# Four graph-transformer layers on one core: sums of the second MLP moved between engines, degrees and a first column read earlier, and branches laid out the other way

## The chip, the cores and the metric

One core of a Trainium2 chip runs the whole program. The metric is the device time of one execution in microseconds. The median of three runs is 3004.81 us (3003.51 to 3010.91). Another execution, of 3007.94 us, was taken by the hardware profiler; all durations come from it. The engines are TensorE (PE; its weight loads are PEld), VectorE (DVE), ScalarE (ACT), GpSimd (POOL) and SyncE (SP, which issues transfers). A name with q (DVEq) is the engine's sequencer, that is, its branches and semaphores.

## The reference

1250 nodes have 512 features; 20,000 edges go from `src` to `dst`. Four layers follow one another; each adds to `x` a graph aggregation and a mixer of the normalised `x`, and then a feed-forward stage of 8 experts with two per node. Layer 0, which the change is about:

```python
xn = _layernorm(x)
x  = x + gnn(xn, edges) + mix(xn)          # mix: 2 x (linear attention; MLP)
x  = x + moe(_layernorm(x))                # gate_w: softmax, top 2 of 8 experts, shared expert
# gnn: deg counts the edges out of a node, plus its loop; dis = rsqrt(deg)
#      relu(segment_sum(dis[row] * dis[col] * (xn @ W.T + b)[row], col))
# mix, MLP i:  y = layernorm(x);  x = x + gelu(y @ W1[i] + b1[i]) @ W2[i] + b2[i]     # 512 -> 2048 -> 512
```

The layers that divide by the incoming degree need its inverse too, which the program computes once, in layer 0.

## The kernel before, in words

**Tiling.** The nodes are ten tiles of 125 rows (`NT`, `TP`), or three chunks of 500, 500 and 250 (`CH`). Everything is float32; matmuls of the aggregation take float32r pairs of a value and its rest.

**The graph.** POOL writes the number of edges between each pair of nodes into DRAM (`adj`) by accumulating transfers during layer 0. `Graph.arrived(t)` (L638 to L647) reads tile t of it into one buffer `at` (L642; issued by POOL), sums its rows to the outgoing degree `degO` on DVE (L643), and adds the tile to `into` on POOL (L645 for the first, L647 for the rest). There is one `at`, so the next read waits until both readers are done. `degrees()` (L649 to L667) makes a flag `heavy` (is any degree over 4096?), the incoming degree `degI` of each node by 20 small matmuls, and its inverse as a row in DRAM: three matmul groups with a row of ones (L664), three clamps and reciprocals on one partition (L665, L666), and three transfers by SP (L667). `inv_sqrt_deg` (L669) makes `dis`, and then the node features `hs` are scaled by it tile by tile on ACT (L1404) and split in two (`parted`, L676).

**The second MLP** is `l0_mlp(1, ..., roomy=False)` (L1205 to L1368), from 957 to 1222 us. It goes in 12 turns: four units of 512 hidden features by three chunks. All but the first turn's hidden product are products of two by two blocks done in seven half-size products (`seven`, L1175; a Strassen-Winograd scheme). `right_sums` (L1168 to L1173) forms four sums of the input's halves, `tx`, for each following turn (11 times, since there is no room to keep them; its other use, on W2, forms `t`). In `seven`, ACT copies three of the products out of PSUM (L1185), two sums are made on DVE (L1194, L1195), and the other products go to four outputs. Of the output products, `outputs` (L1311) adds a kept product to the running `xn` on DVE, and `add_to` (L213) adds the product in PSUM on DVE too. At the end of each turn `aside()` runs one piece of the graph's work, in this order (`steps`): five pieces of two `arrived` each, five pieces of scaling two tiles, then `degrees()`. The program order of each engine is what the source's order and a few pinned places make it; each engine takes its instructions in order.

**Behind the MLP.** `Columns` (L709) reads two tiles' columns of the counts at a time (five reads; the first of them in a pool of its own) by SP. After the MLP, SP issues the first read, then the reads of `x`, with further columns between them, then two weights, and `Arrival` (L462) reads the gate's weights `gw` (L473). `l0_gnn` (L863) then begins with `over` and takes ten tiles: gather by PE, DVE (L868), ACT (L869), DVE (L870), POOL (L871), and the norm and gate of the tile before (L486 to L497).

**Branches.** `over` (L745), called once in each of the four layers, is the path for counts that float32r can't hold: it loads the flag into each engine (L748) and branches (L749) over a body that never runs with this data. Its body's length differs by layer and engine. `Experts.run` has one such branch per layer too (L413), for more tiles of experts than usual. In the built program every engine first compares and, where the flag is 0, jumps over the body to an else block, which sets semaphores for those that wait for the body, and from there goes on.

Of the kernel before, what the change touches and what calls it, by code (L numbers as in the profile page):

```python
# [19 lines left out]
P = 128  # L20
# [4 lines left out]
E = 8  # L25
# [32 lines left out]
def gps_d4_kernel(ctx: ExitStack, tc: tile.TileContext, a: dict, out: bass.AP):  # L58
# [301 lines left out]
    class Experts:  # L360
# [45 lines left out]
        def run(self, to, use, last=lambda: None):  # L406


            self.to = to
            use(range(self.often), self.each(0, self.often))  # L410
            last()
            used = nc.values_load(self.exi[0:1, NLOAD:NLOAD + 1], min_val=2 * NPAIR, max_val=NTI)
            with tc.If(used > self.often + NPAIR):  # L413
                self.most = NLOAD
                self.start()
                use(range(self.often, NLOAD), self.each(self.often, NLOAD))
# [45 lines left out]
    class Arrival:  # L462

        def __init__(self, n, gate, xT=None, hidden=None):

            self.scope = ExitStack()
            self.pool = pool = self.scope.enter_context(tc.tile_pool(name="arrival", bufs=1, side="right"))
            self.rows = dram.tile([T, D], F32, name=f"rows{n}")  # L470
            self.k = gate.shape[0] // P
            self.gw = pool.tile([P, self.k, E], F32, name="gw")
            nc.sync.dma_start(self.gw, gate.rearrange("(c p) e -> p c e", p=P))  # L473
            self.xT, self.hidden = xT, hidden
            self.ps = bank()
            self.turned = None
# [76 lines left out]
    class Graph:  # L553
# [84 lines left out]
        def arrived(self, t):  # L638

            order = tc.keep_in_program_order  # L640
            at = self.at
            move(nc.gpsimd, at, adj[t * TP * T:(t + 1) * TP * T, :].rearrange("(p d) o -> p (d o)", d=T))  # L642
            order(nc.vector.tensor_reduce(degO[:, t:t + 1], at, AX.X, OP.add))  # L643
            if t == 0:
                nc.gpsimd.tensor_copy(self.into, at)  # L645
            else:
                nc.gpsimd.tensor_tensor(self.into, self.into, at, op=OP.add)  # L647

        def degrees(self):  # L649
            most = S.small.tile([TP, 1], F32, tag="most", name="most")  # L650
            nc.vector.tensor_reduce(most, degO, AX.X, OP.max)
            ps = bank()
            nc.tensor.transpose(ps[:1, :TP], most, ident[:TP, :TP])
            one = S.small.tile([1, 1], F32, tag="one", name="one")
            nc.vector.tensor_reduce(one, ps[:1, :TP], AX.X, OP.max)
            nc.vector.tensor_scalar(heavy, one, 4096.0, None, op0=OP.is_gt)
            ps = bank()
            for d in range(NT):
                mm(ps[:TP, d:d + 1], [(self.into[:, tok(d)], ones[:TP, 0:1])])
            nc.vector.tensor_copy(degI, ps[:TP, :NT])  # L660
            for c0, cn in CH:
                ps = bank()
                mm(ps[:1, :cn], [(ones[:TP, 0:1], self.into[:, c0:c0 + cn])])
                inv = S.small.tile([1, 500], F32, tag="inv", name="inv", bufs=1)  # L664
                nc.vector.tensor_scalar(inv[:, :cn], ps[:1, :cn], 1.0, None, op0=OP.max)  # L665
                nc.vector.reciprocal(inv[:, :cn], inv[:, :cn])  # L666
                nc.sync.dma_start(inv_row[:, c0:c0 + cn], inv[:, :cn])  # L667

    def inv_sqrt_deg(deg, r):  # L669

# [71 lines left out]
        nc.sync.dma_start(inv, bass.AP(tensor=inv_row.tensor, offset=inv_row.offset, ap=[[0, P], [1, T]]))  # L742
        return inv

    def over(use, rows=None, xn=None, given=None):  # L745


        some = nc.values_load(heavy[0:1, 0:1], min_val=0, max_val=1)  # L748
        with tc.If(some > 0):  # L749
            W = 500 if rows is None else TP  # L750
            with tc.tile_pool(name="over", bufs=1) as pool:
                more = [given(pool)] if given is not None else []

                def rest(s, c0, cn):
                    at = pool.tile([TP, W], F32, tag="at", name="at")
                    nc.sync.dma_start(at[:, :cn], counts()[:, s, c0:c0 + cn])
                    hi = pool.tile([TP, W], I32, tag="hi", name="hi")
                    nc.vector.tensor_scalar(hi[:, :cn], at[:, :cn].bitcast(I32), -4096, None, op0=OP.bitwise_and)
                    lo = pool.tile([TP, W], F32R, tag="lo", name="lo")
                    nc.vector.tensor_tensor(lo[:, :cn], at[:, :cn], hi[:, :cn].bitcast(F32), op=OP.subtract)  # L760
                    return lo

                def flags(s, k):
                    return dict(start=(s == 0 and k == 0), stop=(s == NT - 1 and k == 1))

                if rows is not None:
                    for d in range(NT):
                        ps = bank()
                        for s in range(NT):
                            lo = rest(s, d * TP, TP)  # L770
                            for k in range(2):
                                nc.tensor.matmul(ps[:TP, :], lo, rows[:, s, k, :], **flags(s, k))
                        use(d, ps[:TP, :])
                for c0, cn in CH if rows is None else []:
                    for f in range(NC):
                        part = part_feature(pool, xn, f, "part")
                        ps = bank()
                        for s in range(NT):
                            lo = rest(s, c0, cn)
                            for k in range(2):  # L780
                                nc.tensor.matmul(ps[:, :cn], part[:, s, k, :], lo[:, :cn], **flags(s, k))
                        use(f, c0, cn, ps[:, :cn], *more)
# [78 lines left out]
        return yT, z  # L861

    def l0_gnn(columns, rows, dis, hs, xn):  # L863
        over(lambda d, ps: add_to(hs[:, d, :], ps), rows=rows)
        for t in range(NT):
            ps = columns.gather(t, rows)
            u = S.small.tile([TP, D], F32, tag="u", name="u")
            nc.vector.tensor_tensor(u, ps, hs[:, t, :], op=OP.add)  # L868
            nc.scalar.activation(u, u, AF.Relu, scale=dis[:, t:t + 1])  # L869
            nc.vector.tensor_tensor(x[:, t, :], x[:, t, :], u, op=OP.add)  # L870
            nc.gpsimd.tensor_tensor(x[:, t, :], x[:, t, :], xn[:, t, :], op=OP.add)  # L871
            arrival[0].step(t)
        arrival[0].step(NT)
# [291 lines left out]
        v.tensor_tensor(o[:, 2], a12, o[:, 1], op=OP.subtract)  # L1165
        v.tensor_tensor(a21, a11, a21, op=OP.subtract)

    def right_sums(o, b11, b12, b21, b22, last=None):  # L1168
        v = nc.vector
        v.tensor_tensor(o[:, 0], b12, b11, op=OP.subtract)  # L1170
        v.tensor_tensor(o[:, 1], b22, o[:, 0], op=OP.subtract)
        v.tensor_tensor(o[:, 2], b21, o[:, 1], op=OP.subtract)
        v.tensor_tensor(b12 if last is None else last, b22, b12, op=OP.subtract)  # L1173
# [31 lines left out]
    def l0_mlp(i, xm, yT, front, then=None, aside=lambda: None, roomy=True):  # L1205

        b2 = row_bc(a["L0_mix_b2"][i])
        H2 = D // 2
        with tc.tile_pool(name=f"mlp{i}", bufs=1) as mp:
            tx = mp.tile([P, 4, 2, T // 2], F32, name="tx") if roomy else None  # L1210

            class Unit:
# [20 lines left out]
            def sums(u, c0, cn):  # L1233
# [3 lines left out]
                if u == 0:  # L1237
                    front.need(c0 + cn)
                if u == 0 or not roomy:
                    right_sums(t, yT[:, 0:2, left], yT[:, 0:2, right], yT[:, 2:4, left], yT[:, 2:4, right], t[:, 3])  # L1240
                return t

            def rests(u, k):
# [53 lines left out]
            def outputs(unit, c0, cn, hT):  # L1297
# [4 lines left out]
                for j in range(n // TP):  # L1302
# [5 lines left out]
                    def out(q):  # L1308
                        def f(ps, more=None):
                            if more is not None:  # L1310
                                nc.vector.tensor_tensor(parts[q], parts[q], more, op=OP.add)  # L1311
                            add_to(parts[q], ps)
                        return f

# [55 lines left out]
    def layer0_mixers():  # L1370
# [3 lines left out]
        with tc.tile_pool(name="l0a", bufs=1) as pool:  # L1374
# [16 lines left out]
            with tc.tile_pool(name="gnn", bufs=1) as gp:  # L1391
                rows = gp.tile([TP, NT, 2, D], F32R, name="hs2")
                dis = S.small.tile([TP, NT], F32, tag="dis", name="dis")
                with tc.tile_pool(name="columns", bufs=1) as cp:
                    graph.fetch(cp)

                    def steps():
                        for t in range(NT):
                            graph.arrived(t)
                            if t % 2:  # L1400
                                yield
                        inv_sqrt_deg(degO, dis)
                        for t in range(NT):
                            tc.keep_in_program_order(nc.scalar.mul(hs[:, t, :], hs[:, t, :], dis[:, t:t + 1]))  # L1404
                            parted(rows[:, t, 0, :], rows[:, t, 1, :], hs[:, t, :])
                            if t % 2:
                                yield
                        graph.degrees()
                        yield

                    pieces = steps()
                    l0_mlp(1, xn, yT, second[1], None, lambda: next(pieces, None), roomy=False)
                    with tc.tile_pool(name="columns2", bufs=1) as cp2:
                        columns = Columns(cp2, cp)
                        columns.fetch(pinned=True)
                        x = ctx.enter_context(tc.tile_pool(name="rows", bufs=1, side="right")).tile([TP, NT, D], F32, name="x")
                        load_x(nc.sync, x, True, lambda **k: columns.fetch(**k))
                        soon["L0"] = [load_w(a["L0_ffn_sw1"], pinned=True), load_w(a["L0_ffn_sw2"], pinned=True)]
                        arrival[0] = Arrival(0, a["L0_ffn_gate_w"], xnT)
                        l0_gnn(columns, rows, dis, hs, xn)  # L1420

    SQD = 512.0 ** 0.5
# [797 lines left out]
```

## Time and profile before

| quantity | value |
|---|---|
| median of three runs | 3004.81 us (3003.51 to 3010.91) |
| profiled execution, and its span | 3007.94 us, 3006.2 us |
| granted clock of PE, mean | 0.952 |
| second MLP | 957 to 1222 us |
| `arrived` reductions (L643) | 973.7 to 1076.4 us |
| first matmul behind the first general-path branch | 1227.54 us |
| branches L749 | near 1223, 1596, 2384 and 2703 us |
| L413, four branches | 1406 to 2964 us |

A line of groups gives the line of the source, engine, operation, output and inputs (partitions x elements), how often, and then busy time in total, mean ns of one, idle time of the engine just before, and what ended most of it. A line of waits reads: engine, tile and line that waited, `<-` what came last, total us, times, longest us. A line of windows gives the stretch, its length, the busy time of each engine with the number of its instructions, the granted clock, the busy share of the DMA engines and GB/s. The view of one source line gives each operation's count, minimum, median and maximum ns, and the start of the first and last, and then who waited for that line. "ns" there, us elsewhere.

### The profile page before, as it was taken

The numbers are of one execution on the slowest core, as the hardware profiler recorded it, in microseconds if no ns is written. First come the engines' busy times: TensorE is split into PE (matmuls) and PEld (weight loads), VectorE is DVE, ScalarE is ACT, GpSimd is POOL, SyncE is SP. The second block draws the span as 40 slices with busy tenths as digits, with TensorE's granted clock in tenths as the row PEclk, the third lists the DMA queues.
The fourth block names the chain that finished last, engine by engine and source line by source line (L and its number), as shares of the span: only waits on it lengthen the run. The fifth ranks groups of instructions, "written<-read, shape, count | busy, mean of one in ns | idle before, by whom it ended". The sixth has DMA issues, their size and how long they took to land. (4 is left out here: it accounts for less than half of the span.)

```text
span 3006.2 us, 33629 instructions
## 1 busy us (share of the span) xinstructions
PE 2753.6 (92%) x12041; PEld 1876.9 (62%) x12041; DVE 1421.4 (47%) x3477; ACT 763.0 (25%) x1715; POOL 673.0 (22%) x496
## 2 busy tenths in 40 slices
PE   7999999999999999889999978999799998889893
PEld 4457778865586878656475556667454657545562
DVE  6835677673356887444541550000324135443523
ACT  3233333342233333120211531111131022320010
POOL 3444444444000300042310001000201002032123
PEclk9999999999999999899999988999899998999897
DMA  8411112111000210638620018775340016651296
GB/s 238 122 15 15 3 29 47 29 33 15 15 15 24 87 45 15 161 108 263 164 77 1 21 35 300 249 239 195 94 132 15 1 35 207 204 145 44 61 317 196
DMA packets 248445, 301.59 MB, mean 100 GB/s; under 512 B 105258, under 2 KB 142509, under 8 KB 248247
## 3 DMA queue, kind: packets, MB, share of 16 engines
q1 hardware_dynamic: 137303, 208.28, 22.2%
q0 software_dynamic: 97408, 66.17, 9.7%
q10 hardware_dynamic: 13536, 24.65, 2.2%
q8 instruction: 106, 1.74, 0.2%
q14 instruction: 92, 0.75, 0.1%
HBM read 253.68 MB, written 44.91 MB: 99 GB/s over the span
## 5 line engine op out<-in xcount | busy, mean ns | idle before, releaser
L627 POOL DMA_INDIRECT adj<-count,cell x160 | 323.7, 2023 | 356.6 <-DMA adj<-count,cell 319.7
L187 PE MATMUL ps<-xnT,w 128*128 128x500 f32 (+1 forms) x832 | 311.7, 528 | 4.0 <-DVEq L749 3.3
L187 PE MATMUL ps<-w,hT 128*128 128x512 f32 (+1 forms) x592 | 264.7, 596 | 3.8 <-ACT hT L1504 3.8
L187 PE MATMUL ps<-w,xnT 128*125 128x512 f32 x560 | 251.5, 598 | 1.5 <-ACT xnT L1657 1.5
L187 PEld LDWEIGHTS ps<-xnT,w 128*128 128x128 f32 x832 | 158.2, 193 | 143.6 <-issue 133.2
L187 PE MATMUL ps<-xgT,w 128*128 128x256 f32 (+1 forms) x1256 | 235.8, 346 | 2.6 <-issue 1.8
L187 PEld LDWEIGHTS ps<-xgT,w 128*128 128x128 f32 x1256 | 208.8, 194 | 44.7 <-issue 19.9
L383 POOL DMA_INDIRECT xg<-rows,r_idx x94 | 89.5, 952 | 561.0 <-PE ps L424 300.5
L187 PEld LDWEIGHTS ps<-w,hT 128*128 128x128 f32 (+1 forms) x592 | 109.5, 190 | 125.3 <-issue 116.5
L425 DVE COPY xgT<-ps 128x512 f32<-128x512 f32 x94 | 61.9, 686 | 253.4 <-PE ps L424 253.4
L187 PEld LDWEIGHTS ps<-w,xnT 128*125 128x125 f32 x560 | 102.0, 189 | 115.0 <-issue 112.2
L444 POOL DMA_INDIRECT came<-yd,slots x80 | 100.1, 1252 | 294.7 <-ACT one L453 101.4
L434 DVE TENSOR_TENSOR y<-ps,erow 128x512 f32<-128x512 f32 x71 | 49.1, 691 | 199.3 <-PE ps L187 192.5
L1185 ACT COPY p<-ps 125x256 f32<-125x256 f32 (+2 forms) x252 | 86.9, 348 | 220.3 <-PE ps L1181 203.7
L1181 PE MATMUL ps<-w,hT 128*125 128x256 f32 x480 | 118.5, 380 | 1.0 <-ACT p L1185 1.0
L213 DVE TENSOR_TENSOR xn<-ps,xn 125x256 f32<-125x256 f32 (+1 forms) x180 | 79.6, 448 | 77.7 <-PE ps L187 55.5
L1805 ACT ACTIVATE hT<-ps,b 128x256 f32<-128x256 f32 (+1 forms) x112 | 48.8, 435 | 262.6 <-PE ps L187 247.8
L187 PE MATMUL ps<-hs,AT 125*125 125x512 f32 x400 | 104.6, 419 | 9.4 <-DVEq L749 9.4
L1181 PEld LDWEIGHTS ps<-w,hT 128*125 128x125 f32 x480 | 88.8, 188 | 14.3 <-ACT p L1185 1.8
L187 PEld LDWEIGHTS ps<-hs,AT 125*125 125x125 f32 x400 | 77.8, 198 | 29.6 <-DVEq L749 10.1
L187 PE MATMUL ps<-AT,part 125*128 125x500 f32 (+1 forms) x480 | 92.5, 355 | 0.0
L187 PEld LDWEIGHTS ps<-AT,part 125*128 125x128 f32 x480 | 79.4, 189 | 13.3 <-issue 0.8
(449 smaller groups left out, 4814.2 us busy)
## 6 DMA issues: line engine op xcount, KB each, us to landing
w<-in_L_ffn_we_dram SPq DMA_DIRECT2D x56, 1024.0 KB
w<-in_L_ffn_w_dram SPq DMA_DIRECT2D x58, 512.0 KB
yd<-y ACTq DMA_DIRECT2D x94, 256.0 KB
w<-in_L_mix_W_dram SPq DMA_DIRECT2D x16, 1024.0 KB
w<-in_L_ffn_w_dram SPq DMA_DIRECT2D x44, 256.0 KB
AT<-adj SPq DMA_DIRECT2D x20, 546.9 KB
rows<-z SPq DMA_DIRECT2D x40, 224.0 KB
keyrow<-keys SPq DMA_DIRECT2D x16, 546.9 KB
```

The source lines that it names most:

```text
L187: nc.tensor.matmul(o, l, r, start=(i == 0), stop=(i == n - 1))
L213: nc.vector.tensor_tensor(dst, ps, dst, op=OP.add)
L383: nc.gpsimd.indirect_dma_start(g, None, self.rows, bass.IndirectOffsetOnAxis(ap=self.idx[:, t:t + 1], axis=0))
L425: nc.vector.tensor_copy(xgT[:, :, j * SL:(j + 1) * SL], ps.rearrange("p (c s) -> p c s", c=NC))
L434: nc.vector.tensor_tensor(y, ps, bias, op=OP.add)
L444: nc.gpsimd.indirect_dma_start(y, None, yd, bass.IndirectOffsetOnAxis(ap=slots[n][:, k * NT + t:k * NT + t + 1], axis=0))
L627: nc.gpsimd.indirect_dma_start(adj, bass.IndirectOffsetOnAxis(ap=self.cell[:, c:c + 1], axis=0), self.count[:, c:c + 1], None, compute_op= ...
L1181: nc.tensor.matmul(banks[b], ls(k), rs(k), start=first and k == 0, stop=k == 1, skip_group_check=True)
L1185: nc.scalar.copy(o, banks[b])
L1805: nc.scalar.activation(hT[f // NC][:, f % NC, :ns], ps[:, :ns], AF.Gelu, bias=b1[:, f:f + 1])
```

## The change

1. In the second MLP only, the four sums of `tx` (11 groups) and the sum of a kept product with `xn` (60 instructions) are issued to GpSimd. The sums for W2 and those inside `seven` remain on DVE.
2. `degO` is summed by an ACT copy of `at` into itself with an accumulating output. The addition to `into` on POOL reads what ACT wrote.
3. `degrees()` and `inv_sqrt_deg` follow right behind the last `arrived`; the scaling of `hs` comes after them. The inverse row is made by transposing `degI` (125x10) once on PE, one clamp and one reciprocal of 10x125 on DVE, and one transfer.
4. The first read of columns is issued by SP behind `degrees()`, in the middle of the MLP; the other reads have their pool as before. `gw` is read before the MLP into a tile of its own.
5. `over` loads the flag once, at its first call, and keeps it in registers for the other three. For layer 3 its path by rows goes by chunks of up to four tiles, for layer 0 by single tiles as before; in layer 3 the body's DVE instructions fall from 400 to 128.
6. Both kinds of branch are built with the other block next in line: the compare falls through to the else block's semaphores, and then an unconditional jump leads over the body.

The instructions of the program as built, before and after, bodies that never run included: PE 9252 and 9254, DVE 5818 and 5414, ACT 2445 and 2488, POOL 854 and 955, SP 2743 and 2583.

```diff
@@ Experts.run @@
-            with tc.If(used > self.often + NPAIR):
+            with tc.If(used > self.often + NPAIR, preferred_fallthrough_block=False):
@@ Arrival.__init__ @@
-            self.gw = pool.tile([P, self.k, E], F32, name="gw")
-            nc.sync.dma_start(self.gw, gate.rearrange("(c p) e -> p c e", p=P))
+            self.gw = gw
+            if gw is None:
+                self.gw = pool.tile([P, self.k, E], F32, name="gw")
+                nc.sync.dma_start(self.gw, gate.rearrange("(c p) e -> p c e", p=P))
@@ Graph.arrived @@
-            order(nc.vector.tensor_reduce(degO[:, t:t + 1], at, AX.X, OP.add))
+            order(nc.scalar.activation(at, at, AF.Copy, accum_out=degO[:, t:t + 1]))
@@ Graph.degrees @@
-            for c0, cn in CH:
-                ps = bank()
-                mm(ps[:1, :cn], [(ones[:TP, 0:1], self.into[:, c0:c0 + cn])])
-                inv = S.small.tile([1, 500], F32, tag="inv", name="inv", bufs=1)
-                nc.vector.tensor_scalar(inv[:, :cn], ps[:1, :cn], 1.0, None, op0=OP.max)
-                nc.vector.reciprocal(inv[:, :cn], inv[:, :cn])
-                nc.sync.dma_start(inv_row[:, c0:c0 + cn], inv[:, :cn])
+            ps = bank()
+            nc.tensor.transpose(ps[:NT, :TP], degI, ident[:TP, :TP])
+            inv = S.small.tile([NT, TP], F32, tag="inv", name="inv", bufs=1)
+            nc.vector.tensor_scalar(inv, ps[:NT, :TP], 1.0, None, op0=OP.max)
+            nc.vector.reciprocal(inv, inv)
+            nc.sync.dma_start(inv_row.rearrange("o (t p) -> (o t) p", p=TP), inv)
@@ over @@
-        some = nc.values_load(heavy[0:1, 0:1], min_val=0, max_val=1)
-        with tc.If(some > 0):
-            W = 500 if rows is None else TP
+        if "some" not in soon:
+            soon["some"] = nc.values_load(heavy[0:1, 0:1], min_val=0, max_val=1)
+        with tc.If(soon["some"] > 0, preferred_fallthrough_block=False):
+            W = chunks[0][1]
@@ l0_gnn @@
-        over(lambda d, ps: add_to(hs[:, d, :], ps), rows=rows)
+        over(lambda d, ps: add_to(hs[:, d, :], ps), rows=rows, chunks=ONE)
@@ right_sums @@
-    def right_sums(o, b11, b12, b21, b22, last=None):
-        v = nc.vector
+    def right_sums(o, b11, b12, b21, b22, last=None, v=nc.vector):
@@ l0_mlp @@
+            beside = nc.vector if roomy else nc.gpsimd
...
-                    right_sums(t, yT[:, 0:2, left], yT[:, 0:2, right], yT[:, 2:4, left], yT[:, 2:4, right], t[:, 3])
+                    right_sums(t, yT[:, 0:2, left], yT[:, 0:2, right], yT[:, 2:4, left], yT[:, 2:4, right], t[:, 3],
+                               beside)
...
-                                nc.vector.tensor_tensor(parts[q], parts[q], more, op=OP.add)
+                                beside.tensor_tensor(parts[q], parts[q], more, op=OP.add)
@@ layer0_mixers @@
                     graph.fetch(cp)
+                    columns = Columns(None, cp)
+                    gw = S.small.tile([P, NC, E], F32, tag="gw", name="gw", bufs=1)
+                    nc.sync.dma_start(gw, a["L0_ffn_gate_w"].rearrange("(c p) e -> p c e", p=P))
...
                         inv_sqrt_deg(degO, dis)
+                        graph.degrees()
+                        yield
+                        columns.fetch(pinned=True)
                         for t in range(NT):
                             tc.keep_in_program_order(nc.scalar.mul(hs[:, t, :], hs[:, t, :], dis[:, t:t + 1]))
                             parted(rows[:, t, 0, :], rows[:, t, 1, :], hs[:, t, :])
                             if t % 2:
                                 yield
-                        graph.degrees()
-                        yield
...
-                        columns = Columns(cp2, cp)
-                        columns.fetch(pinned=True)
+                        columns.pool = cp2
...
-                        arrival[0] = Arrival(0, a["L0_ffn_gate_w"], xnT)
+                        arrival[0] = Arrival(0, a["L0_ffn_gate_w"], xnT, gw=gw)
```

## The prediction

> **What bounds the kernel now.** Read first the busy table, then the clock and the windows, then the waits of TensorE where the diff bites, then the two branch lines. PE is busy 92% of the span at a granted clock of 0.952, and the change takes no matmul from the general stream, so a gain can only come out of the 8% in which PE stands, in the places touched: the second MLP of layer 0 (957 to 1222 us), the general-path branches, and the first tiles of the layer-0 aggregation. The page:
> ```profile
> PE 2753.6 (92%) x12041; PEld 1876.9 (62%) x12041; DVE 1421.4 (47%) x3477; ACT 763.0 (25%) x1715; POOL 673.0 (22%) x496
> ```
> The windows (us, then busy time of each engine, clock, DMA share, GB/s) cut the stage in the count stretch, the quiet rest, and the first tiles behind the branch:
> ```profile
> 960.00:1080.00 120.00, 114.94 (x565) 95.03 (x564) 105.67 (x206) 41.62 (x103) 34.31 (x28) 1.00 0.28 87
> 1080.00:1222.00 142.00, 135.46 (x687) 117.05 (x685) 113.73 (x263) 55.35 (x128) 0.00 (x0) 1.00 0.08 25
> 1222.00:1260.00 38.00, 24.23 (x86) 18.90 (x85) 9.24 (x19) 5.38 (x9) 3.83 (x3) 0.78 0.93 238
> ```
> The reader is to see that DVE, not PE, is the fullest engine after PE there (105.7 of 120, 113.7 of 142), that POOL does 34 us in the count stretch and nothing in the quiet one, and that PE stands 14 of 38 us after the branch. What PE waits for (total, times, longest), from 940 to 1235 us, and then from 1222 to 1262:
> ```profile
> PE ps L1181 <- DVE xn L213: 5.6, 5, 1.6
> PE ps L187 <- DVEq L749: 5.2, 1, 5.2
> PE ps L1181 <- ACT p L1185: 3.7, 4, 1.3
> PE ps L1181 <- DVE sh L1164: 1.8, 1, 1.8
> ```
> ```profile
> PE ps L187 <- DMA gw<-in_L_ffn_gate_w_dram: 6.0, 1, 6.0
> PE ps L187 <- DVEq L749: 5.2, 1, 5.2
> PE ps L193 <- DVE z L491: 2.5, 1, 2.5
> ```
> So the full DVE costs PE only 5.6 + 1.8 + 0.4 us in the whole MLP. This caps what relief of DVE can bring. The branch and gw are as large as that together.
>
> **Count stretch: sums to POOL, the reduction to ACT.** On DVE, L643 is 10 x 1.445 = 14.5 us, the tx sums (L1170 to L1173) 7 x 4 x 0.67 + 4 x 4 x 0.41 = 25.4, L1311 60 x 0.43 = 25.9; 65.8 us of DVE go. POOL has no such row. Its 125x512 sum takes 1.29 (L871), so by elements 128x500 is 1.25, 128x250 and 125x256 are 0.65: 28 x 1.25 + 16 x 0.65 + 60 x 0.65 = 84 us, estimated. But POOL runs in order, and its adds wait for transfers:
> ```profile
> L647 POOL TENSOR_TENSOR at<-at 125x1250 f32<-125x1250 f32 x9 | 23.4, 2596 | 34.9 <-DMA at<-adj 34.9
> L643 DVE TENSOR_REDUCE degO<-at 125x1 f32<-125x1250 f32 x10 | 14.5, 1446 | 0.3 <-DMA at<-adj 0.2
> ```
> Today reduction and add start together on landing. ACT's new pass writes `at` in place, so the add now waits for the landing and then for ACT. ACT shows no 125x1250 pass; its L1404 pass 125x512 is 0.72, and its 128x250 and 128x500 copies 0.36 and about 0.6, which by size makes 1.3 to 1.75; I take 1.3. POOL's account for the 120 us: 34.3 busy now, 34.9 + 5.8 waiting (L647, and L645's 5.8), ten ACT passes 13, six tx groups (four of width 500, two of 250) 4 x 5.0 + 2 x 2.6 = 25, and the 21 sums of L1311 that ran there 14. Sum 127 us in 120: POOL is over-full by 7, and a tx group or kept sum queued behind a landing comes as late as one tile, up to 4.1 + 1.3 + 2.4 = 8 us; the product that reads it holds PE. ACT likewise stands before its pass until the landing, with the PSUM copies of L1185 behind it. Against that, the 4.0 us of PE's waits for L213 in this stretch may go. **+7, bounds -4 and +15** (the upper end is two tiles' lateness exposed).
>
> A lock between the engines weighs in. L1195 takes 0.42 us, but 2.56 when it starts beside POOL's add (988.56, add 988.46 to 990.85); the maximum shows here:
> ```profile
> L1195 DVE TENSOR_TENSOR p<-p,p x42: 265/416/2565, 976.3 to 1219.4; 125x256 f32<-125x256 f32 x20, 128x250 f32<-128x250 f32 x14, 128x125 f32<-128x125 f32 x8
> L1311 DVE TENSOR_TENSOR xn<-xn,p x120: 403/424/1949, 404.8 to 1220.4; 125x256 f32<-125x256 f32 x120
> ```
> A sum moved to POOL is thus not fully beside what DVE keeps (L1194, L1195, L1163 to L1166); the bound above covers that. The Trainium skill, "SBUF — State Buffer", section "Who interferes with whom", states the same against this change and in harder terms: a DVE instruction with two SBUF inputs and a GpSimd one that reads SBUF shut each other out for a whole instruction, but a reduction does not contend. Taken literally, all of POOL's estimated 84 us would block those DVE instructions, and L643, which leaves, never was part of that conflict; the sum would then lie at the slow end.
>
> **Quiet rest.** POOL is empty there: 5 tx groups and 39 kept sums fit in 142 us. But a kept sum stands between ACT's copy (L1185) and L213's update; on POOL it is 0.65 for 0.42, some 0.25 us late at ten or so turns of a product, 2.5 us at most, and 1.5 more for locked DVE. The two waits DVE causes there (1.8 and 1.6) may go. **+1, bounds -3 and +4.**
>
> **Degrees.** Three matmul groups (2.26 us of PE from 1195.16) become one transpose (L653's 125x125 row: 0.27); the transpose waits for degI (DVE's L660 stood 1.5 us behind PE), unless a product is ready between. Reciprocals 8.2 us of DVE become one row of 10x125, hidden. The inverse row's DMAs go from three to one, off the path. hs scaling comes after, ACT 7.2 + 6.2 us with 60 us of cover; it was ready long before. **-1.5, bounds -2.3 and 0.**
>
> **Branches.**
> ```profile
> L749 PEldq COMPARE_BRANCH  x4: 341/1884/3449, 1221.8 to 2696.1; - x4
> L749 DVEq COMPARE_BRANCH  x4: 56/60/76, 1223.0 to 2702.9; - x4
> L749 DVEq EVENT_SEMAPHORE  x4: 21/21/21, 1227.5 to 2705.8; - x4
>   PE ps L187: 16.1, 4
> ```
> DVE takes 0.06 us to branch and signals 4.4 us later at the first place (1223.0 to 1227.5), 2.9 at the last: the jump over the body itself. PE lost 16.1 us at four places, behind that signal. In the new order the semaphore stands ahead of the far jump, so PE no longer waits for DVE's. But PE has a jump of its own, until now beside its draining matmuls, and now after its drain: 0.34 or 3.45 us by its own four rows. First place: 5.2 lost now, 0.5 to 3.9 then, so -4 if short, -1 if long. The other three lost 10.9 together: second and third 3.3 each, and a long jump costs 3.4, so 0; if short, -3 each. Last: 4.3, -2.6 to -0.5. The four L413 branches wait for experts' results, 0.2 at most. I take -3, 0, 0, -2: **-5, bounds -12.5 and -1.** Loading the flag once drops three reads of 0.3 to 0.55 us per engine that stand beside PE's work. Against this, the Trainium skill's "Advanced Engine Details and Errata", "Control Flow Timing", gives a compare-and-branch 108 ns; the row shows 0.06 us for it and 4.4 until the target runs. "Runtime: NRT & Kernel Launch", "Instruction fetch mechanics", says why such a figure may fail: a jump out of the loaded window waits for a fetch. By 0.1 us for each jump the branches would give the full -12.5; the rows speak against it.
>
> **gw and columns.** gw is issued at 1243.30 behind x and columns and lands at 1254.6, with PE waiting 6.0 us; now it is there from the start. PE's next bound is the norm chain (2.5 us wait for z just before) and columns that arrive at 248 GB/s: 1.5 of it I let come back. **-4.5, bounds -6 and -2.** SP's far jump (1213.6 to 1218.2, 4.6 us) lay beside the MLP's end. Now the x and AT issues that follow 1222.4 stand behind it, at a DMA share of 0.93. The first column is already loaded, so only the third gather may see it: **+1, bounds 0 and +4.**
>
> **Sum.** 7 + 1 - 1.5 - 5 - 4.5 + 1 = -2.0 us against the profiled run of 3007.9, which is 3.1 above the median 3004.8: 3005.9 profiled, **3003** as a median.
>
> **Rivals.**
> - *The work balances* (chance 0.27): POOL's landing waits fall where no product needs it; -4 - 3 - 2.3 - 6 - 5.5 + 0 = -20.8, 2984. For: DVE 105.7 of 120 is nearly full, and POOL idle 78%. Against: PE's waits on DVE are 7.8 us in all.
> - *POOL becomes the bound* (0.24): its queue stands at every landing and the tx group behind it makes PE wait, from the point where its account passes the stretch by more than one tile's lateness (8 us; I have 7); two tiles' lateness exposed +15, +4, degrees -1, branches -2, gw -3, SP +2: +15, 3020.
> - *The branch edit does nothing* (0.07): PE's own jump replaces DVE's wait, -1 for -5: 3007.
> - The forecast (0.42), 2994 to 3012.
>
> **Numbers.** A measurement of this kernel can tell about 0.3%, 9 us, from no change: under 2995.8 is faster, over 3013.8 slower. Of the forecast's 0.42 I give 0.09 to faster and 0.03 to slower; with the first rival faster is 0.36, with the second slower 0.27; the rest, 0.37, is no change. All ends at once would be -27.8 and +20; the range stops at the rivals, 2982 to 3021.
>
> **What would show it.** POOL's L647 waits move from the DMA to ACT's degO, with spacing of adds near 9 us instead of 7.6; PE's waits in 960 to 1080 name POOL's tx or xn (wrong if they fall below 4 us). The wait for DVEq at the branch goes, and PE restarts under 1 us or about 3.5 after its last matmul. No wait for gw; PE idle in 1222 to 1260 falls from 14 to about 7. It is wrong if clock or stages the diff does not touch move.

## The result and the profile after

The changed kernel takes 3051.9 us (3047.0 to 3055.4, four runs) against 3007.9 for the kernel before on the same chip (3003.5 to 3011.3): a ratio of 1.0146 (95% interval 1.0124 to 1.0168), slower by 44 us. The range of the prediction ended at 3021. The profiled execution has a span of 3053.4 us at a clock of 0.946.

Line numbers move: the products of the second MLP are L1186 now (L1181 before), ACT's copies L1190 (L1185), `left_sums` L1169 to L1172 (L1163 to L1166), the two sums inside `seven` L1199 and L1200 (L1194, L1195), tx L1175 to L1178, the kept sum L1318 (L1311), ACT's pass L645, POOL's add L649, the branch L752, z L493 (L491).

The busy table of the page, of the kernel after:
```profile
PE 2769.6 (91%) x12036; PEld 1885.5 (62%) x12036; DVE 1388.3 (45%) x3359; ACT 775.1 (25%) x1735; POOL 765.8 (25%) x600
```
POOL is 93 us busier, but DVE only 33 us less busy, though 65.8 us of its work have left by the prediction's own count: what DVE keeps lasts longer. The first of `left_sums`, before 669 ns on average in this stretch (L1163), is one example (957 to 1262 us):
```profile
L1169 DVE TENSOR_TENSOR sh<-hT 128x500 f32<-128x500 f32 x8 | 10.8, 1348 | 2.3 <-ACT hT L1291 2.3
```
And PE is 16 us *more* busy, with the same matmuls but for those of the degrees. The windows around the whole second MLP, first of before, then of after (length, then busy time of PE, PEld, DVE, ACT, POOL, then granted clock):
```profile
957.80:1222.40 264.60, 252.96 (x1255) 213.02 (x1253) 221.60 (x472) 96.97 (x231) 35.49 (x30) 1.00 0.17 53
```
```profile
956.20:1259.60 303.40, 268.42 (x1250) 223.42 (x1248) 185.93 (x353) 109.29 (x251) 128.70 (x134) 0.94 0.15 46
```
The stage grew by 38.8 us. PE stood 264.6 - 253.0 = 11.6 us before and 303.4 - 268.4 = 35.0 after: 23.3 us more. The other 15.5 are in the matmuls themselves, at a clock of 0.94 in place of 1.00. Windows of after show how: just ahead of the second-longest wait (6.0 us, to 1020.92) and in the 13 us behind it, then behind a wait of 2.0 us (to 993.86) and one of 3.0 (to 1051.92):
```profile
1010.00:1014.00 4.00, 4.00 (x20) 3.45 (x20) 4.00 (x2) 0.81 (x3) 4.00 (x3) 1.00 0.84 260
1021.00:1024.50 3.50, 3.50 (x9) 2.73 (x10) 0.64 (x2) 0.37 (x1) 0.63 (x1) 0.50 0.42 144
1024.50:1028.00 3.50, 3.50 (x15) 2.89 (x14) 1.49 (x4) 0.37 (x1) 1.45 (x2) 0.86 0.00 0
1028.00:1034.00 6.00, 6.00 (x29) 5.09 (x28) 3.94 (x10) 2.35 (x5) 2.59 (x4) 1.00 0.00 1
994.80:998.20 3.40, 3.40 (x9) 2.64 (x8) 1.00 (x3) 0.93 (x3) 0.72 (x1) 0.50 0.00 0
1052.00:1055.50 3.50, 3.50 (x11) 2.88 (x12) 3.50 (x3) 1.06 (x4) 3.50 (x2) 0.62 0.00 0
```
For 4.6 us behind the wait of 6.0 the clock is at 0.50 (a 128x256 matmul takes 0.63 us and starts every 0.43, instead of 0.38 and 0.22), and then 1.00 again: 2.3 us more. Six waits of PE in this stage are of 3.0 us or longer, and behind each the clock is at 0.50 for 3.0 to 5.9 us. Two more stretches of 3.4 us follow the wait of 2.0 and the twenty one-column matmuls of the degrees (1117.7 to 1121.1). Before, the longest wait was 1.8 us, and the clock 1.00 throughout. What PE stood for, of after, 955 to 1262 us (total, times, longest):
```profile
PE ps L1186 <- DVE xn L213: 21.7, 7, 6.3
PE ps L1186 <- POOL tx L1176: 9.2, 3, 3.1
PE ps L1186 <- DVE hT L1286: 2.2, 3, 0.9
PE ps L187 <- SPq L752: 0.9, 1, 0.9
```
For L213 on DVE PE waits four times as long as before (5.6 us). The branch takes 5.2 us for DVEq before and 0.9 now; that this is not so in every execution is shown below.

Behind the branch the two traces, matmul by matmul, are 33 us apart, 27 at the first gate product (gw gave 6.5), 36 at z of a later tile, 38 at 1315 us of before, 33 at 1330, in the routing of experts, 42 behind it (1340 and 1350 us), and 46 at the end.

### The profile page after: what moved, and what is told of

It is laid out like the page before. It is cut to its first block, busy times and chain, and to the rows that moved or that the text cites. A ratio compares the mean times of both kernels' runs of the same rounds, so it can differ in the third digit from the quotient of the medians.

```text
span 3053.4 us, 33674 instructions
## 1 busy us (share of the span) xinstructions
PE 2769.6 (91%) x12036; PEld 1885.5 (62%) x12036; DVE 1388.3 (45%) x3359; ACT 775.1 (25%) x1735; POOL 765.8 (25%) x600
## 5 line engine op out<-in xcount | busy, mean ns | idle before, releaser
L383 POOL DMA_INDIRECT xg<-rows,r_idx x94 | 89.3, 950 | 555.9 <-PE ps L424 299.6
L1190 ACT COPY p<-ps 125x256 f32<-125x256 f32 (+2 forms) x252 | 86.6, 348 | 242.3 <-PE ps L1186 215.9
L213 DVE TENSOR_TENSOR xn<-ps,xn 125x256 f32<-125x256 f32 (+1 forms) x180 | 80.6, 450 | 100.7 <-PE ps L187 53.0
L1186 PE MATMUL ps<-w,hT 128*125 128x256 f32 x480 | 120.2, 385 | 0.5 <-ACT p L1190 0.5
L1186 PEld LDWEIGHTS ps<-w,hT 128*125 128x125 f32 x480 | 90.7, 192 | 14.3 <-ACT p L1190 0.9
```

The source lines that it names most:

```text
L213: nc.vector.tensor_tensor(dst, ps, dst, op=OP.add)
L383: nc.gpsimd.indirect_dma_start(g, None, self.rows, bass.IndirectOffsetOnAxis(ap=self.idx[:, t:t + 1], axis=0))
L1186: nc.tensor.matmul(banks[b], ls(k), rs(k), start=first and k == 0, stop=k == 1, skip_group_check=True)
L1190: nc.scalar.copy(o, banks[b])
```

## The experiments

All ratios are to runs of the kernel before on the same chip. Read from them, 0.001 is 3.0 us.

| kernel | tx sums | kept sums | reduction | ratio (95%) | MLP, us | PE stands, us | clock there |
|---|---|---|---|---|---|---|---|
| before | DVE | DVE | DVE | 1 | 264.6 | 11.6 | 1.00 |
| after | POOL | POOL | ACT | 1.0146 (1.0124 to 1.0168) | 303.4 | 35.0 | 0.94 |
| kept_dve | POOL | DVE | ACT | 1.0149 (1.0111 to 1.0186) | 299.6 | 33.3 | 0.94 |
| red_dve | POOL | POOL | DVE | 1.0117 (1.0091 to 1.0144) | 296.5 | 31.7 | 0.95 |
| quiet_only | half | half | ACT | 1.0063 (1.0036 to 1.0089) | 281.1 | 22.4 | 0.98 |
| tx_dve | DVE | POOL | ACT | 1.0056 (1.0034 to 1.0078) | 275.1 | 17.6 | 0.98 |
| tx_twice | DVE, twice | DVE | ACT | 1.0053 (1.0034 to 1.0072) | 284.2 | 23.2 | 0.97 |
| sums_dve | DVE | DVE | ACT | 1.0016 (1.0000 to 1.0032) | 265.4 | 13.0 | 0.99 |
| rest | DVE | DVE | DVE | 1.0005 (0.9991 to 1.0019) | 262.9 | 10.4 | 0.99 |

The last three columns are of each one's profiled execution, which for after and tx_twice was the slowest of its runs and for kept_dve the fastest.

**Which move costs.** The first theory (Q) was that of the prediction: a sum on POOL is late, since it stands in order behind a landing or behind other sums. The rival (L): whenever POOL sums, it shuts out DVE's sums of two operands in SBUF, whoever waits for whom.

*tx_dve*, the tx sums back on DVE:
```diff
-                    right_sums(t, ..., t[:, 3],
-                               beside)
+                    right_sums(t, ..., t[:, 3])
```


> The change with the tx sums back on DVE; the kept sums stay on POOL and the reduction on ACT. Theory Q (POOL's order: a sum is late because it stands behind a landing or behind other sums): the three waits of PE for tx (9.2 us) go, and with them most of the three long waits for L213 that had a tx group ahead on POOL (6.2, 6.4 and 4.3 us): 20 to 28 us less than the change, about 3028, and the clock in the stage rises. Theory L (POOL's sums shut DVE out whenever they run): POOL's added time falls from 95 to 43 us, so about half of the loss goes: 3030, with L1169 and L1199 still longer than before.

Measured 3023.3 us: by the ratio 27 of the 44 are gone, near Q's number (20 to 28) and more than L's half.

*kept_dve*, the kept sums back on DVE:
```diff
-                                beside.tensor_tensor(parts[q], parts[q], more, op=OP.add)
+                                nc.vector.tensor_tensor(parts[q], parts[q], more, op=OP.add)
```


> The change with the kept sums (L1318) back on DVE; the tx sums stay on POOL and the reduction on ACT. Theory Q: the waits for L213 (21.7 us in seven places) fall to about 5, the three waits for tx (9.2 us) stay: about 20 us less than the change, 3031. Theory L: POOL's time falls by 43 of 95 us: 15 to 20 less, 3034.

Measured 3049.3, no gain at all. Theory Q fails here in the place it was surest of: the kept sum and `add_to` are both on DVE, nothing of them waits in POOL's queue, and PE's wait for L213 is 19.1 us in five places, not 5. Theory L's number, 15 to 20 us less, fails too: the loss does not go by POOL's busy time alone. The kept sums cost 0.0040 alone on POOL (tx_dve less sums_dve), and nothing beside the tx sums (after less kept_dve). What the tx sums do, the timeline of kept_dve shows (start us, us, engine, line, operation; `...` for lines left out):
```profile
1004.39 1.51 POOL L1175 TENSOR_TENSOR tx<-xnT 128x500 f32<-128x500 f32 x1
1004.89 1.56 DVE L1172 TENSOR_TENSOR w<-w 128x512 f32<-128x512 f32 x1
...
1005.86 1.69 POOL L1178 TENSOR_TENSOR tx<-xnT 128x500 f32<-128x500 f32 x1
1006.37 1.73 DVE L1171 TENSOR_TENSOR s<-w,s 128x512 f32<-128x512 f32 x1
1007.51 1.51 POOL L1176 TENSOR_TENSOR tx<-xnT,tx 128x500 f32<-128x500 f32 x1
1008.02 1.29 DVE L1199 TENSOR_TENSOR p<-p,p 125x256 f32<-125x256 f32 x1
...
1009.23 1.87 DVE L1318 TENSOR_TENSOR xn<-xn,p 125x256 f32<-125x256 f32 x1
1009.55 1.25 POOL L1177 TENSOR_TENSOR tx<-xnT,tx 128x500 f32<-128x500 f32 x1
```
Each DVE sum runs beside one of POOL and ends 0.3 to 0.55 us behind it: 1.56 and 1.73 us for a sum of 0.68, 1.29 and 1.87 for one of 0.42. The ends alternate, one instruction of each engine. So beside four sums on POOL four on DVE last 6.5 us in place of 2.2, on DVE's in-order way to the next L213, for which PE then waits 6.2 us (to 1013.01).

*red_dve*, the reduction back on DVE:
```diff
-            order(nc.scalar.activation(at, at, AF.Copy, accum_out=degO[:, t:t + 1]))
+            order(nc.vector.tensor_reduce(degO[:, t:t + 1], at, AX.X, OP.add))
```


> The change with the reduction back on DVE; the sums stay on POOL. Theory Q: each add starts at the landing instead of 1.3 us behind it, ten times, so POOL's queue is 13 us shorter in the count stretch: 5 to 12 us less than the change, about 3043. Theory L: the adds run beside DVE as before and DVE has 14 us more to do: 3052 to 3058. Theory A: ACT is what is late: 15 us less or more, 3035.

3045.1: some 9 us (0.0029) less than the change, with intervals that overlap. Between Q's and L's numbers for it, nearer to Q's: the pass ahead of the add is a small term, not the cause.

*sums_dve* is both of the first two edits together, *rest* all three.

> The change with all sums back on DVE; only the reduction stays on ACT. Theory Q and theory L alike: the loss of the second MLP, 37 us, goes but for ACT's stand at the landings, 0 to 6 us: 3008 to 3014. A third theory, A (ACT's pass in front of the add and ACT standing there hold the PSUM copies): 15 us or more stay, 3022.

> The change with all sums and the reduction back on DVE: degrees early, one transpose, early gw and first column, branches. If the loss is all in the moves between engines, this is 2 to 10 us under the kernel before (branches -7, matmuls of the degrees -2, gw -6, given back by late transfers +6 to +9): 2998 to 3005. If the early columns or degrees cost something themselves, it is over 3010.

3012.3 and 3008.5, so rest lacks the 2 to 10 us of gain that were expected of it. The sums are 0.0130 of the 0.0146. ACT's pass costs 0.0011, which these intervals can't tell from nothing; theory A is out. Of the rest of the change nothing is left to see, see below.

*quiet_only* has the sums on DVE in the first six turns, on POOL in the last six, when no counts arrive:
```diff
+                if not roomy and q == 5:
+                    beside[0] = nc.gpsimd
```


> The change with the sums on DVE in the first six turns (while counts arrive) and on POOL in the last six; the reduction stays on ACT. No sum on POOL stands behind a landing. If the landings make the loss, it falls to the two tx waits (3.3 each) and the wait behind a tx group (4.3) of that part: 10 to 14 us over the version without moved sums, about 3016. If only the waits behind landings count, 3006. Theory L: half of the sums stay, and so half of the loss: 3025.

3030.5 (ratio to before 1.0063, 19 us), above all the numbers expected and nearest to theory L's 3025. Of the 0.0130 that the sums cost, 0.0047 arises in turns without a single landing, so POOL's sums are dear without landings. How much of the 0.0083 of the first six turns is due to landings, no run separates.

**The lock by itself.** The first try put 216 extra sums of 128x200 on POOL into a tile that nobody else reads:
```diff
+                if not roomy and q > 5:
+                    for _ in range(36):
+                        nc.gpsimd.tensor_tensor(idle, idle, idle, op=OP.add)
```


> The kernel before, and in addition 216 sums of 128x200 on POOL, into a tile that nobody else reads, behind the sixth to the last turns of the second MLP: they wait for nobody, and nobody waits for them. Theory Q: nothing is late, so the time stays within 5 us of the kernel before. Theory L: DVE's sums with two operands in SBUF start late or last longer for some 120 us of POOL's work; the waits of PE for DVE grow by 15 us or more, and the clock falls: over 3020.

It came to 3079.1 (1.0228, 1.0204 to 1.0252), but proves little: the extra sums ran early, between the reads of counts, and DVE's reduction L643 stood 36.3 us behind those. In the next pair program order holds them behind the last add:
```diff
+                if not roomy and q > 5:
+                    for _ in range(24):
+                        tc.keep_in_program_order(nc.gpsimd.tensor_tensor(idle, idle, idle, op=OP.add))
```
and in the other `for _ in range(48)` with `nc.gpsimd.memset(idle, 0.0)`.

> The kernel before, and in addition 144 sums of 128x200 on POOL (about 0.6 us each) behind its last add of the counts, held there by program order, into a tile that nobody else reads or waits for. Unlike in the first try, no read of the counts stands behind them. Theory L (POOL's sums shut out DVE's two-operand sums): for some 90 to 110 us DVE's sums of 0.42 to 0.69 us last 0.9 to 1.4, PE waits 15 us or more for DVE and the granted clock of that stretch falls under 0.95: 3025 or more. Theory Q (only what stands behind POOL is late): within 5 us of before.

> The same with 288 fills of 128x200 on POOL in place of the 144 sums: POOL is as busy, but reads nothing from SBUF. Theory L: DVE's sums last as long as before and the time is within 5 us of the kernel before. If it is POOL's being busy, its writes or its instructions that hurt, it is as slow as with the sums.

With sums 3030.3, a ratio of 1.0076 (1.0055 to 1.0096); with fills 3007.9, 1.0001 (0.9985 to 1.0017). POOL is busy 94.0 us with the sums, 76.4 with the fills. Groups on DVE by form, from 1080 to 1170 us (count, busy us, mean ns), of the kernel with sums:
```profile
L1311 DVE TENSOR_TENSOR xn<-xn,p 125x256 f32<-125x256 f32 x19 | 11.7, 625 | 1.2 <-ACT p L1185 0.9
L213 DVE TENSOR_TENSOR xn<-ps,xn 125x256 f32<-125x256 f32 x26 | 10.0, 414 | 2.3 <-PE ps L1181 2.2
L1195 DVE TENSOR_TENSOR p<-p,p 125x256 f32<-125x256 f32 x6 | 4.0, 663 | 0.6 <-ACT p L1185 0.6
```
and of the one with fills:
```profile
L213 DVE TENSOR_TENSOR xn<-ps,xn 125x256 f32<-125x256 f32 x27 | 11.1, 420 | 3.3 <-PE ps L1181 2.8
L1311 DVE TENSOR_TENSOR xn<-xn,p 125x256 f32<-125x256 f32 x19 | 7.8, 421 | 1.2 <-ACT p L1185 0.9
L1195 DVE TENSOR_TENSOR p<-p,p 125x256 f32<-125x256 f32 x6 | 2.5, 424 | 0.1
```
Same shape, same engine, same neighbour: L1311 with two operands in SBUF grows from 421 to 625 ns beside POOL's sums, L213 with one in PSUM stays at 414 to 420, and a POOL that only writes disturbs neither. What PE stands for in the kernel with sums (960 to 1222 us), where nobody waits for POOL's new work:
```profile
PE ps L1181 <- DVE xn L213: 13.1, 9, 3.7
PE ps L1181 <- DVE hT L1279: 6.6, 5, 2.2
```
This shows theory L's mechanism: 94 us of POOL's sums cost 23 us (by the ratio) with no dependence at all.

**How much is length.** A tx group on POOL also lasts twice as long. *tx_twice* does every tx sum twice on DVE (the same numbers again), so that a group is as long and no lock is added:
```diff
+        for _ in range(2 if again else 1):
             v.tensor_tensor(o[:, 0], b12, b11, op=OP.subtract)
```
and so for the other three.

> The change with all sums on DVE and the reduction on ACT, and in it each of the 44 tx sums done twice on DVE, the second writing the same numbers: a tx group then lasts 5.4 us as on POOL, without a lock. Theory Q2 (a tx group on POOL is late because it lasts twice as long): the three waits for tx are there (3 each, then for DVE), the kept sums stand behind the groups: 25 to 37 us over the version with the sums once on DVE, which was 3012. Theory L (the lock is the larger part): 6 to 15 us over it, 3018 to 3027.

3027.4, that is 0.0037 or 11 us over sums_dve, as theory L had it; PE's waits for tx are there (4.8 us in three places), now for DVE. tx on POOL cost 0.0133 or 40 us (kept_dve less sums_dve). So a quarter or so is the length of the group and the rest comes only with POOL. The difference holds all that follows, the clock too, and is not a clean measure of the lock.

**Branches, gw, and what takes their place.** *branches* is the kernel before with the new order in both branches and the flag loaded once:
```diff
-            with tc.If(used > self.often + NPAIR):
+            with tc.If(used > self.often + NPAIR, preferred_fallthrough_block=False):
...
-        with tc.If(some > 0):
+        with tc.If(soon["some"] > 0, preferred_fallthrough_block=False):
```

> The kernel before with only the branches changed: the ordinary case next in line and the flag loaded once. By the trace of the change, the first branch gives 4.4 us and the last 2.5, the other two nothing since PE's own far jump takes 3.5 us: 6 to 7 us less than before, about 3000. If the x reads behind SP's own far jump come too late, 2 to 4 us less.

3012.4 (1.0004, 0.9989 to 1.0019): no gain. PE's waits of branches, from 1222 to 1345 us:
```profile
PE ps L187 <- DMA gw<-in_L_ffn_gate_w_dram: 8.5, 1, 8.5
PE ps L193 <- DVE z L491: 6.8, 2, 4.2
PE ps L285 <- DVE r_m L280: 6.6, 1, 6.6
PE ps L187 <- DMA AT<-adj: 4.7, 1, 4.7
```
The wait of 5.2 us for DVEq is gone, and at the same place stand 4.7 for the first columns, which are only read there; PE's wait for gw is 2.5 us longer. DVE's jump had covered the first columns. With the column read early PE waits 0.9 us there in after, but 3.8 in rest (`issue`, below). There PE's own jump decides: 0.3 to 0.4 us in after, kept_dve, red_dve and quiet_only, 3.3 to 3.9 in rest, sums_dve, tx_dve, tx_twice and late_gw. One and the same kernel has both: PE waits 4.2 us in rest_z and 0.9 in rest_z5. So the 0.9 of after is in part luck; what decides it stays open.

*late_gw* is rest with the gate weights read late again:
```diff
-                    gw = S.small.tile([P, NC, E], F32, tag="gw", name="gw", bufs=1)
-                    nc.sync.dma_start(gw, a["L0_ffn_gate_w"].rearrange("(c p) e -> p c e", p=P))
...
-                        arrival[0] = Arrival(0, a["L0_ffn_gate_w"], xnT, gw=gw)
+                        arrival[0] = Arrival(0, a["L0_ffn_gate_w"], xnT)
```

> The version with all sums and the reduction on DVE again, and in it the gate weights read late as before. In the trace of that version the early weights gave 8.6 us at the first gate product, and 7 came back at the tile whose z waits for the writes of rows. If that exchange is the rule, the late weights cost nothing: the wait for gw (6 to 8 us) is there again, the wait for z of 8 us goes, and the time is within 4 us of that version, 3005 to 3012. If the early weights are worth their wait, it is 6 us slower, 3014.

3009.6 (1.0002, 0.9985 to 1.0020), as rest. PE's waits from 1215 to 1345 us, of rest:
```profile
PE ps L193 <- DVE z L493: 13.9, 3, 7.8
PE ps L187 <- issue: 3.8, 1, 3.8
PE ps L187 <- DVE r_ohl L337: 3.6, 1, 3.6
```
and of late_gw:
```profile
PE ps L187 <- DMA gw<-in_L_ffn_gate_w_dram: 12.1, 1, 12.1
PE ps L193 <- DVE z L493: 6.8, 2, 4.2
```
12.1 us for gw and 6.8 for z in the one, 13.9 for z and none for gw in the other. z of a tile has three buffers, and in rest DVE's next one stands for the write of an older one to `rows` (the trace names `rows<-z`, 2.1 us). This write is behind columns and weights in SP's queue: a z made at 1234.1 us is issued by SP at 1251.5 only. The rest of PE's 7.8 us is program order: in rest DVE does the next tile's sums and norm (1255.4 to 1260.5) ahead of this z, where before each z stands right behind its own norm. *rest_z* hands these writes to POOL:
```diff
-            move(nc.sync, self.rows[tok(t), :], z)
+            move(nc.sync if self.xT is None else nc.gpsimd, self.rows[tok(t), :], z)
```


> The version with all sums and the reduction on DVE again, with layer 0's writes of z to rows issued by POOL in place of SP, so that they don't stand behind SP's reads of columns and weights. If SP's queue is what z waits for, the 7.8 us wait goes and the time falls by 4 to 7 us, to 3002. If the transfers themselves are late (they share the DMA engines), the wait stays: 3008.

> The version with all sums and the reduction on DVE and layer 0's writes of rows issued by POOL, once more with more rounds: it was 5 us under the kernel before with an interval that held no change. If it is faster, the ratio stays near 0.9985 with an interval under 1; if that was chance, it comes to 1.000.

3005.3 (0.9988, 0.9970 to 1.0005), and again with more rounds 3005.4 (0.9986, 0.9974 to 0.9997): 4 us under the kernel before, the only version with an interval (the second) that lies under 1, by less than half of what the prediction called telling. The waits for z fall from 13.9 to 6.3 us in the one execution and to 8.9 in the other.

## Why the prediction was wrong, by its own steps

- **What bounds the stage: right, and not followed.** The cap (DVE costs PE only 7.8 us in all) was not contradicted: no version's MLP is more than 1.8 us shorter than before. It spoke against any gain from the move, and the forecast's sum was +8 for the MLP. The stage took 38.8.
- **Lock: the step that failed.** "A sum moved to POOL is thus not fully beside what DVE keeps [...]; the bound above covers that." It did not. The row of 2.56 us for 0.42 was read rightly, but its price was 1.5 us in the quiet rest and nothing in the count stretch, whose +7 came from POOL's queue alone. The runs show in its place: POOL gets some 93 us of sums (its busy time in the stage goes from 35.5 to 128.7), a DVE sum beside one of them lasts about as long as that (625 ns beside 653 in lock_sums), and 94 us of sums that nobody waits for cost 23 us. How much of the 38.8 us is the lock alone is not measured; tx_twice puts the longer tx groups at about a quarter of what tx on POOL costs. The Trainium skill, "SBUF — State Buffer", section "Who interferes with whom", had said that such instructions shut each other out for the whole of one and that a reduction does not contend, and the prediction named this as the slow end but did not price it. The runs agree with it: sums hold, fills don't (421 ns beside them), an operand in PSUM is free (414), and the reduction L643 took 1.44 to 1.46 us before, beside POOL's adds.
- **POOL's queue over-full by 7 us: too small, and its cause not borne out.** Up to the `tx,s` product that starts at 1065.2 us before and 1079.7 after, the stage had already lost 16.0 us, more than the upper bound of 15. But POOL's waits at L649 and L647 for ACT are 30.9 us against 40.7 for the transfers before, and quiet_only loses 0.0047 without landings. The rival "POOL becomes the bound" (3020 us) had the direction right, but from this same cause.
- **Quiet rest, +1: wrong by an order.** Behind that product, where only the last counts still land, the stage lost the other 22.8 us. Two terms were too small or missed: the lock, and that in the turns without outputs between (three in the stage) the next hidden product waits for tx, 9.2 us, of them 6.2 here.
- **Clock: missing from the sum**, though a moving clock was among the signs of being wrong. 15.5 of the 38.8 us are slower matmuls. The six waits of 3.0 us and more cost 1.5 to 3 each at half the clock, 13 together (an estimate from the lengths of the stretches). In the table the clock falls as PE's standing grows. The Trainium skill, "TensorE: Matmul & The Clock Gate", section "What's actually happening", states that an idle window of about 3.4 us halves the clock and a busy one restores it. The stretches of 3.4 and 6.8 us in the trace agree with its window, but no idle time of 3.4 us was needed: after a wait of 3.0 us the clock is 0.62 in the next 3.5 us of after (1052.00 to 1055.50), and after one of 2.0 it is 0.50 (994.80 to 998.20), while in red_dve it stays at 1.00 after one of 3.0 (to 987.22). The prediction's +15 for "two tiles' lateness" should have had this on top.
- **Degrees, -1.5: right in size, partly by luck.** The MLP of rest is 262.9 us against 264.6. But PE is only 0.5 us less busy there: the three groups (2.26 us) are gone, yet right behind the twenty one-column matmuls the clock is at 0.50 from 1092.0 to 1095.4, which costs 1.7 us; before, at the same matmuls (1193 us), it stays at 1.00. The other 1.2 us are less standing.
- **Branches, -5: right at the place, worth nothing in the end.** First place 5.2 to 0.9 (3.8 in rest: both of the prediction's cases, short and long, occur), second and third no gain, since PE's own far jump takes its place (3.5 us). The view of the branch line, of after:
```profile
L752 PEldq COMPARE_BRANCH  x8: 64/205/3501, 1259.1 to 2753.7; - x8
  PE ps L187: 10.1, 4
```
  16.1 us became 10.1. The rival "the branch edit does nothing" was right in time, by another way: transfers and the next stage's order take the gain.
- **gw, -4.5: gave 6.5, and it all came back.** "1.5 of it I let come back" was the mis-sized part; z, which waits for its older write and stands later in DVE's order, takes the rest. In the routing of experts, 3.7 us for r_m (L280) became 0.4, and 3.6 for r_ohl (L337) came in its place.
- The last 4 us or so, from 42 at 1350 us to 46 at the end, lie in later layers. PE's waits for xn (L205) rise there from 15.2 to 19.2; in rest they are 19.7. The cause stays open.

## What to carry to other kernels

Before a sum with both operands in SBUF goes to GpSimd, count the sums of that kind that VectorE keeps beside it: each of them then lasts about as long as the GpSimd sum beside it, and a VectorE that is 84% busy but seldom waited for, as here, is better left alone. A wait of TensorE that grows past 3 us cost 1.5 to 3 us more in the clock here. Price a move by the waits of the engine that bounds the stage, not by the busy time that it frees. A wait taken away by an earlier load or a shorter jump was worth here only its distance to the next thing waited for, so look what lands or comes in order there next.

## What the runs showed of the hardware

VectorE's and GpSimd's sums of two SBUF operands alternate instruction by instruction: a sum of 0.42 us took up to 1.87 in one group of tx, and 3.1 us at most in the kernel after; beside fills on GpSimd (265 ns each) VectorE's sums of two SBUF operands keep their 421 ns, and its sums with a PSUM operand keep 414 to 420 ns beside either.

PE's far jump at one and the same branch took 3.8 us in one execution of a kernel and 0.4 in another (rest_z, rest_z5).
